# Half products in seven of eight for the last stage of an attention and mixture-of-experts kernel, with a square root by Newton steps

## The chip, the core and the metric

The kernel runs on one core of one Trainium2 chip. The metric is device time in microseconds (us), measured around one launch. A core has five engines with a queue of instructions each: TensorE (PE, the matrix engine; PEld is its weight loading), VectorE (DVE), ScalarE (ACT), GpSimd (POOL) and SyncE (SP, which here only issues DMA transfers). All arithmetic that matters is f32.

## The reference

Input is x of 4 sequences x 1024 tokens x 512 features. The kernel computes one layer in two halves:

```
x = x + layernorm(attention(layernorm(x)))     # linear attention, 16 heads of 32, decay per head, chunks of 128
x = x + layernorm(ffn(layernorm(x)))           # mixture of experts with a shared expert

layernorm(x) = (x - mean) / sqrt(var + 1e-5)
ffn(x):
  shared = (silu(x @ sh_gate.T) * (x @ sh_up.T)) @ sh_down.T       # width 1408
  top 2 of 8 experts by softmax(x @ router.T), weights normalised to sum 1
  cur[e] = (silu(gate_e) * up_e) @ down_e.T                        # width 352, for the chosen tokens
  out = sum of the two cur * weight  +  sigmoid(x @ shared_gate.T) * shared
```

## The kernel before, in words

Tokens are cut into 8 blocks (`n`) of 512 (`TB`), a block into 4 tiles (`j`) of 128. The 512 features are `KC` = 4 slices of 128, the shared expert's width 1408 is `IC` = 11 slices of 128 (`ic`). PE's order of work is written out by hand for the whole kernel (L67); DVE's and ACT's order is written out from L914 on and is chosen by a scheduler before that; POOL's and SP's orders are the program's with the scheduler's changes. Pools of tiles set when a buffer or a PSUM bank can be used again.

The work has five parts, one after the other on PE.

1. **Attention**, blocks 0 to 7 (loop at L614). In the stage of block n PE makes the projections of block n+1 between the chunks of block n, so that they fill its waits. A chunk: scores (`chunk_scores`, products with `sm` made on DVE at L368), output and state (`chunk_out`, bank `pa` from L378 on, `pst` at L400), projection. After chunk 3 comes `attn_residual` (L430): layernorm of the attention's output, on ACT for the scaling (L253), and POOL adds it to `xa` (L435); then `ln2` (L438) and `routing`, whose units (transposes `pt_f`, router logits, choice of experts, scatter of rows to DRAM) are spread over the next block's stage. Transposes `pt_a` (L280) need the normalised next block. In the stage of block 7 there is no next block, and PE does gate and up of the shared expert for block 0 (`shared_units`, L554), whose weights `up_weights` (L139) brings chunk by chunk and whose `xT` waits for the transfer from `xTd`. In front of it `xa` is loaded on the same queue, SP.
2. Down of block 0, and then the shared expert for block 1 (loop from L790, weights by `up_weights`, down weights at L792), during which the experts' weights (`wx`, 23 MB on ACT's queue) are loaded. Both blocks' results go to DRAM (`earlyd`).
3. **Routed tiles**: `NX` = 71 tiles of 128 rows sorted by expert (L881). Each is read from `xg`, transposed, multiplied with its expert's gate and up (L845, 352 columns), turned (L858), multiplied with down (L867), and written to `yg`. In them POOL has nothing to do.
4. **Last stage**: the shared expert for blocks 2 to 7 (L983). For each block 11 chunks of gate and up into banks `pg` and `pu` (4 + 4 f32 products of 512 columns per chunk, L156), silu on ACT, product `h` on DVE (L163), then down for 4 tiles (L1020, 11 f32 products each). All of the weights stay in SBUF (`kept`, `wdr`). PE's first chunk of block 2 lies between the last routed tiles. As a list of `side` work, spread over a block's chunks by count, DVE has `routed_sum` (L941: gathers the two rows of a token from `yg` by POOL, weighs and adds them; L944, L945), `early_block` (L966: the same for blocks 0 and 1, added to `earlyd`, with statistics), and `finish` of the block before (L950: `rstd_of`, scaling at L128, the addition of x1 on POOL at L957, the output).
5. The last block finishes tile by tile on DVE (`finish` with w = 1), the last tile after PE's last product.

`rstd_of` (L106) serves every layernorm: variance plus eps, square root on ACT (L111), reciprocal on DVE (L113), and one Newton step of four small DVE operations (L116 to L119). In the trace an f32 product counts as two instructions on PE.

Of the kernel before, what the change touches and what calls it, by code (L numbers as in the profile page):

```python
# [42 lines left out]
def tile_sandwich(  # L43
# [62 lines left out]
    def rstd_of(mv, name, w=TPB):  # L106

        ve = small.tile([P, w], F32, tag="ve", name=f"ve_{name}")
        nc.vector.tensor_scalar(ve, mv[:, :, 1], EPS, None, ALU.add)
        sd = small.tile([P, w], F32, tag="sd", name=f"sd_{name}")  # L110
        nc.scalar.activation(sd, ve, AF.Sqrt)  # L111
        rs = small.tile([P, w], F32, tag="rs", name=f"rs_{name}")
        nc.vector.reciprocal(rs, sd)  # L113

        t = small.tile([P, w], F32, tag="nt", name=f"nt_{name}")
        nc.vector.tensor_tensor(t, rs, rs, ALU.mult)  # L116
        nc.vector.tensor_tensor(t, t, ve, ALU.mult)
        nc.vector.tensor_scalar(t, t, -0.5, 1.5, ALU.mult, ALU.add)
        nc.vector.tensor_tensor(rs, rs, t, ALU.mult)  # L119
        return rs  # L120
# [18 lines left out]
    def up_weights(n, ic):  # L139

        f = slice(ic * P, (ic + 1) * P)
        wg = wp.tile([P, KC, P], F32, tag="wg", name=f"wg_{n}_{ic}")
        nc.sync.dma_start(wg, shgv[:, :, f])
        wu = wp.tile([P, KC, P], F32, tag="wu", name=f"wu_{n}_{ic}")
        nc.sync.dma_start(wu, shuv[:, :, f])
        return wg, wu
# [7 lines left out]
    def up_half(dst, w, xT):  # L154
        for kc in range(KC):
            nc.tensor.matmul(  # L156
                dst, lhsT=w[:, kc, :], rhs=xT[:, kc, :], start=(kc == 0), stop=(kc == KC - 1)
            )
# [8 lines left out]
    with ExitStack() as ph:  # L167
# [275 lines left out]
        def routing(n, xn2):  # L443
# [4 lines left out]
            pick = small.tile(two, F32, tag="pick", name=f"pick_{n}")  # L448
            both = small.tile([P, TPB, E], BF16, tag="both", name=f"both_{n}")
            pe = small.tile(two, F32, tag="pe", name=f"pe_{n}")  # L450
# [21 lines left out]
        def choice(n, lgT, pick, both, pe):  # L472
# [8 lines left out]
            nc.scalar.activation(sig[:, n, :], lg[:, :, E], AF.Sigmoid)  # L481
# [72 lines left out]
        def shared_units(n):  # L554
# [4 lines left out]
            w, pg = {}, {}  # L559

            def gate(ic):
                w[ic] = up_weights(n, ic)
                pg[ic] = bank(f"pg_{n}_{ic}")
                up_half(pg[ic], w[ic][0], xT)

            def up(ic):
                pu = bank(f"pu_{n}_{ic}")
                up_half(pu, w[ic][1], xT)
                gated(h[:, ic, :], pg[ic], pu, f"{n}_{ic}")
# [159 lines left out]
        for e in range(1, E):  # L729
            less = small.tile([P, 2 * NTB * TPB], F32, tag="less", name=f"less_{e}")  # L730
# [16 lines left out]
    with ExitStack() as ph:  # L747
        ps = ph.enter_context(tc.tile_pool(name="psf", bufs=2, space=PSUM, reuse_waits="tile"))

# [3 lines left out]

        def routed_tiles(mid):
            wxp = mid.enter_context(tc.tile_pool(name="wxp", bufs=1, reuse_waits="tile"))
# [35 lines left out]
            for ic in range(IC):  # L791
                wg, wu = up_weights(n, ic)  # L792
                wd = xk.tile([P, DM], F32, tag="wd", name=f"wd_{n}_{ic}")
                nc.sync.dma_start(wd, shd[ic * P : (ic + 1) * P, :])
                pg = ps.tile([P, TB], F32, tag="pg", name=f"pg_{n}_{ic}")
                up_half(pg, wg, xT)
                pu = ps.tile([P, TB], F32, tag="pu", name=f"pu_{n}_{ic}")
                up_half(pu, wu, xT)
# [79 lines left out]
            ahead_2 = block_ahead(EARLY), [up_weights(EARLY, ic) for ic in range(2)]  # L878
# [21 lines left out]
            xT, ((wg, wu), _) = ahead_2  # L900
            pg = ps.tile([P, TB], F32, tag="pg", name=f"pg_{EARLY}_0")
            up_half(pg, wg, xT)
            hT = turned(NX - 1, last[0])
            pu = ps.tile([P, TB], F32, tag="pu", name=f"pu_{EARLY}_0")
            up_half(pu, wu, xT)
            rows_out(NX - 1, hT, last[1])
            return *ahead_2, pg, pu


        with ExitStack() as mid:  # L910
            first = routed_tiles(mid)
# [6 lines left out]
        )  # L918
        res = ph.enter_context(tc.tile_pool(name="res", bufs=1, reuse_waits="tile"))
        xk = ph.enter_context(tc.tile_pool(name="xk", bufs=2, reuse_waits="tile"))  # L920
        kept = {i: w for i, w in enumerate(first[1])}
        for ic in range(len(kept), IC):
            f = slice(ic * P, (ic + 1) * P)
            wg = res.tile([P, KC, P], F32, tag=f"wg{ic}", name=f"wgr_{ic}")
            nc.sync.dma_start(wg, shgv[:, :, f])
            wu = res.tile([P, KC, P], F32, tag=f"wu{ic}", name=f"wur_{ic}")
            nc.sync.dma_start(wu, shuv[:, :, f])
            kept[ic] = wg, wu
        wdr = res.tile([P, IC, DM], F32, tag="wdr", name="wdr")

        def gather(n, j, k):
            y = xk.tile([P, DM], F32, tag="y", name=f"y_{n}_{j}_{k}", bufs=11)
# [8 lines left out]
        def routed_sum(n, j):  # L941

            y0, y1 = gather(n, j, 0), gather(n, j, 1)
# [4 lines left out]
            return y0  # L948

        def finish(n, acc, x1, mv, j0, w):  # L950

            rs = rstd_of(mv, f"y{n}_{j0}", w)
            for j in range(w):
                a = acc[:, j0 + j, :]
                normed(a, a, mv, rs, j)
                eng = nc.vector if w == 1 else nc.gpsimd
                eng.tensor_tensor(x1[:, j0 + j, :], x1[:, j0 + j, :], a, ALU.add)  # L957
            nc.sync.dma_start(ov[n][:, j0 : j0 + w, :], x1[:, j0 : j0 + w, :])

        def block_tiles(n):  # L960
            x1 = xk.tile([P, TPB, DM], F32, tag="x1", name=f"x1_{n}")
            nc.sync.dma_start(x1, x1d[n])
            acc = xk.tile([P, TPB, DM], F32, tag="acc", name=f"acc_{n}")
            return x1, acc

        def early_block(n):  # L966

            x1, acc = block_tiles(n)
            nc.sync.dma_start(acc, earlyd[n])
            mv = small.tile([P, TPB, 2], F32, tag="mve", name=f"mve_{n}")  # L970

            def add(j):
                y = routed_sum(n, j)
                nc.vector.tensor_tensor(acc[:, j, :], acc[:, j, :], y, ALU.add)
                stats(mv, j, acc[:, j, :], f"e{n}")

            return [lambda j=j: add(j) for j in range(TPB)] + [
                lambda: finish(n, acc, x1, mv, 0, TPB)
            ]

        behind = []
        xT = first[0]
        for n in range(EARLY, NTB):  # L983
            if n + 1 < NTB:
                xT_next = res.tile([P, KC, TB], F32, tag=f"xT{n % 2}", name=f"xT_{n + 1}")
                nc.sync.dma_start(xT_next, xTd[n + 1])
            h = res.tile([P, IC, TB], F32, tag="h", name=f"h_{n}")
            side = behind
            if n - EARLY < EARLY:
                side = side + early_block(n - EARLY)  # L990
            x1, acc = block_tiles(n)
            ys = [None] * TPB

            def own(j):
                ys[j] = routed_sum(n, j)

            side = side + [lambda j=j: own(j) for j in range(TPB)]
            done = 0
            for ic in range(IC):
                wg, wu = kept[ic]  # L1000
                if n == EARLY and ic == 0:
                    pg, pu = first[2:]
                else:
                    pg = ps.tile([P, TB], F32, tag="pg", name=f"pg_{n}_{ic}")
                    up_half(pg, wg, xT)
                    pu = ps.tile([P, TB], F32, tag="pu", name=f"pu_{n}_{ic}")
                    up_half(pu, wu, xT)
                gated(h[:, ic, :], pg, pu, f"{n}_{ic}")
                if n == EARLY and ic == 3:
                    nc.scalar.dma_start(wdr, shd.rearrange("(k p) f -> p k f", p=P))  # L1010

                start = 4 if n == EARLY else 0
# [89 lines left out]
```

## Time and profile before

| | |
|---|---|
| time, median of 3 runs | 2164.21 us (2162.38 to 2167.74) |
| profiled execution: time | 2165.27 us |
| profiled execution: span | 2163.6 us |
| granted TensorE clock | 0.996 |
| PE busy | 2121.8 us, 98% |
| last stage, PE's first to last instruction | 1482.2 to 2155.8 us |
| HBM traffic | 120.46 MB read, 66.59 MB written |

The span is the time from the first to the last instruction in the trace; the execution's own time is 1.7 us longer. A row of the profile reads: line of the source, engine, operation, result tile <- operand tiles, partitions x elements, type, count | busy us, mean ns of one | idle time of the engine right before, and what ended it. A row of PE's waits gives what it waited for, the us in total, how often, and the longest. In a row of the timeline the first two numbers are start and duration in us from the span's start, x8 a run of eight instructions. Matmul durations overlap (they are pipelined), so what an instruction costs is read from the distance of starts, not from its duration.

### The profile page before, as it was taken

The page shows a single profiled execution, that of the slowest core. Times are in us where ns is not written, and L with a number is a line of the kernel's source. Part 1 is how long each engine was busy: PE and PEld are TensorE (multiplying, and loading weights), DVE is VectorE, ACT ScalarE, POOL GpSimd, SP SyncE. Part 2 cuts the span into 40 slices and gives each one's busy share as a digit, 9 for nine tenths or more (in the row PEclk, how much of TensorE's full clock was granted, in tenths as well). Part 3 has the DMA queues.
Part 4 walks back from the last instruction along what each step waited for, and adds up shares of the span by engine and source line. Part 5 has one row for each costly group of instructions (what it writes and reads, how often), then busy time and mean ns, then how long its engine had stood idle before and what let it go on. Part 6 is the DMA issues. An engine that isn't in the chain of part 4 may idle for free.

```text
span 2163.6 us, 23030 instructions
## 1 busy us (share of the span) xinstructions
PE 2121.8 (98%) x8971; PEld 1100.1 (51%) x8971; DVE 597.6 (28%) x1443; ACT 398.0 (18%) x657; POOL 277.8 (13%) x270
## 2 busy tenths in 40 slices
PE   7999999999989999999999999999999999999998
PEld 3555555555545444456655655654444444444443
DVE  2434444544442320111111111111434211212123
ACT  2223323323221210122222221221111000101010
POOL 1122132132130220000000000002322100101010
PEclk9999999999999999999999999999999999999999
DMA  6011221221232349411222221216623020111000
GB/s 226 20 59 59 98 98 59 78 98 59 98 122 73 107 162 358 146 64 66 66 68 64 63 69 64 64 59 197 230 68 103 20 78 20 56 41 54 10 20 20
DMA packets 101851, 188.54 MB, mean 87 GB/s; under 512 B 8849, under 2 KB 42658, under 8 KB 97266
## 3 DMA queue, kind: packets, MB, share of 16 engines
q1 hardware_dynamic: 80498, 128.00, 17.4%
q0 software_dynamic: 11088, 36.00, 4.9%
q10 hardware_dynamic: 10160, 23.07, 3.1%
q8 instruction: 74, 1.21, 0.2%
q14 instruction: 31, 0.25, 0.0%
HBM read 120.46 MB, written 66.59 MB: 86 GB/s over the span
## 4 chain that ended last, share of the span: by engine, by line
PE 87%; DMA 4%; DVE 4%; POOL 2%; SPq 1%; issue 1%; ACT 1%; ACTq 0%; POOLq 0%; DVEq 0%
PE pu L156 12%; PE pg L156 12%; PE pd L1020 10%; PE pq L306 10%; PE pox L867 8%; PE pgx L845 8%; PE pux L845 8%; PE po L424 5%; PE pv L320 2%; PE pd L587 2%; PE ptx L838 1%; POOL xa L435 1%; PE pa L378 1%; DVE sm L368 1%; DMA wx<-in_wdn_dram 1%; PE pst L400 1%
## 5 line engine op out<-in xcount | busy, mean ns | idle before, releaser
L306 PE MATMUL pq<-xnT,wqkv_sb 128*128 128x512 f32 x512 | 233.2, 601 | 0.0
L1020 PE MATMUL pd<-wdr,h 128*128 128x512 f32 x528 | 227.6, 592 | 0.0
L933 POOL DMA_INDIRECT y<-yg,made x64 | 63.5, 992 | 1030.1 <-DMA wur<-in_shu_dram 682.2
L867 PE MATMUL pox<-wx,hT 128*128 (+1 forms) x426 | 194.8, 593 | 0.0
L163 DVE TENSOR_TENSOR h<-sg,pu 128x512 f32<-128x512 f32 x88 | 60.4, 686 | 463.1 <-PE pu L156 405.5
L162 ACT ACTIVATE sg<-pg 128x512 f32<-128x512 f32 x88 | 52.5, 597 | 703.7 <-PE pg L156 633.7
L845 PE MATMUL pgx<-wx,xtT 128*128 x568 | 179.9, 459 | 1.3 <-ACT xtT L840 1.3
L845 PE MATMUL pux<-wx,xtT 128*128 x568 | 179.8, 460 | 0.0
L1020 PEld LDWEIGHTS pd<-wdr,h 128*128 128x128 f32 x528 | 100.5, 190 | 126.1 <-issue 126.1
L156 PE MATMUL pg<-xT,wgr 128*128 128x512 f32 x360 | 161.9, 593 | 0.0
L156 PE MATMUL pu<-xT,wur 128*128 128x512 f32 x360 | 161.9, 592 | 0.0
L306 PEld LDWEIGHTS pq<-xnT,wqkv_sb 128*128 128x128 f32 x512 | 95.4, 192 | 109.2 <-issue 105.8
L845 PEld LDWEIGHTS pgx<-wx,xtT 128*128 128x128 f32 x568 | 107.4, 189 | 80.3 <-issue 33.2
L860 DVE COPY hT<-pth 128x256 f32<-128x256 f32 x71 | 30.2, 425 | 362.6 <-PE pth L858 362.6
L845 PEld LDWEIGHTS pux<-wx,xtT 128*128 128x128 f32 x568 | 102.6, 191 | 45.1
L320 PE MATMUL pv<-wqkv_sb,xnT 128*128 128x512 f32 x256 | 117.3, 601 | 0.0
L424 PE MATMUL po<-wo_sb,aT 128*128 128x512 f32 x256 | 115.7, 595 | 0.0
L156 PEld LDWEIGHTS pg<-xT,wgr 128*128 128x128 f32 x360 | 68.5, 190 | 86.0 <-issue 86.0
L156 PEld LDWEIGHTS pu<-xT,wur 128*128 128x128 f32 x360 | 68.5, 190 | 86.0 <-issue 83.6
L867 PEld LDWEIGHTS pox<-wx,hT 128*128 128x128 f32 (+1 forms) x426 | 75.8, 191 | 68.5 <-issue 68.3
L313 ACT ACTIVATE qk<-pq,bqk_sb 128x512 f32<-128x512 f32 x64 | 44.0, 687 | 261.5 <-PE pq L306 261.5
L350 POOL TENSOR_TENSOR qd<-qk,decq 128x512 f32<-128x512 f32 x28 | 35.5, 1268 | 433.6 <-PE pa L388 407.4
(204 smaller groups left out, 2241.7 us busy)
## 6 DMA issues: line engine op xcount, KB each, us to landing
xt<-xg SPq DMA_DIRECT2D x71, 256.0 KB, 2.6
yg<-yt SPq DMA_DIRECT2D x71, 256.0 KB, 2.0
wx<-in_wgu_dram ACTq DMA_DIRECT2D x8, 1408.0 KB, 12.9
xa<-in_x_dram SPq DMA_DIRECT2D x8, 1024.0 KB, 5.2
x1d<-xa SPq DMA_DIRECT2D x8, 1024.0 KB, 3.9
xTd<-xT SPq DMA_DIRECT2D x8, 1024.0 KB, 4.7
x<-x1d SPq DMA_DIRECT2D x8, 1024.0 KB, 6.0
xn<-in_x_dram SPq DMA_DIRECT2D x7, 1024.0 KB, 6.1
```

Of the source, the lines that this page charges most:

```text
L156: nc.tensor.matmul(dst, lhsT=w[:, kc, :], rhs=xT[:, kc, :], start=(kc == 0), stop=(kc == KC - 1))
L162: nc.scalar.activation(sg, pg, AF.Silu)
L163: nc.vector.tensor_tensor(h, sg, pu, ALU.mult)
L306: nc.tensor.matmul(pq, lhsT=wqkv_sb[:, kc, oc * P : (oc + 1) * P], rhs=xnT[:, kc, :], start=(kc == 0), stop=(kc == KC - 1),)
L313: nc.scalar.activation(qk[:, oc, :], pq, AF.Identity, bias=bqk_sb[:, oc : oc + 1])
L320: nc.tensor.matmul(pv, lhsT=xnT[:, kc, j * P : (j + 1) * P], rhs=wqkv_sb[:, kc, 2 * DM : 3 * DM], start=(kc == 0), stop=(kc == KC - 1),)
L424: nc.tensor.matmul(po, lhsT=aT[:, g, :], rhs=wo_sb[:, g, :], start=(g == 0), stop=(g == G - 1))
L587: nc.tensor.matmul(pd[j], lhsT=h[:, ic, j * P : (j + 1) * P], rhs=wa[:, ic, :] if ic < 8 else wb[:, ic - 8, :], start=(ic == 0), stop=(ic ...
L845: nc.tensor.matmul(dst, lhsT=xtT[:, kc, :], rhs=wx[:, bass.ds(off + (kc * 2 * IM + o), IM)], start=(kc == 0), stop=(kc == KC - 1),)
L867: nc.tensor.matmul(po, lhsT=hT[:w, c, :], rhs=wx[:w, bass.ds(off + (WG + c * DM), DM)], start=(c == 0), stop=(c == 2),)
L933: nc.gpsimd.indirect_dma_start(out=y, out_offset=None, in_=yg[:, :], in_offset=bass.IndirectOffsetOnAxis(ap=made[:, k, n, j : j + 1], axis=0),
L1020: nc.tensor.matmul(pd, lhsT=h[:, ic, j * P : (j + 1) * P], rhs=wdr[:, ic, :], start=(ic == 0), stop=(ic == IC - 1),)
```

## The change

It has six parts.

**Seven products of eight (Winograd's form of Strassen's scheme).** In the last stage each large product is a two by two block product. Gate and up of a chunk: rows are gate and up, the inner cut is features 0 to 255 against 256 to 511, the columns are tokens 0 to 255 against 256 to 511 of the block. Down: rows are token halves, inner halves are chunks 0 to 4 against 5 to 9 with chunk 10 split in its own way, columns are halves of 256 features. Instead of 8 half products there are 7, on sums of blocks; four sums of weights and four sums of tokens (or hidden values) go in, and DVE adds the products up: in `sums` (`q`, `u`, `c2`), and `gb` or `c12` in the end. The first PSUM halves pass through ACT (`copied`). The chunk's instructions are split in `begin`, `middle` and `end`, and chunk i+1's `begin` stands on PE ahead of chunk i's `end`. The scheme uses banks `pa` (3 buffers), `pb` (2), `pd` (3).

**Where the sums are made.** Sums of gate and up weights: on POOL in block 7's attention stage, as the weights pass through (`weight_sums`), written to DRAM as `w8d`; from there every later chunk's weights come in one transfer, in the last stage three buffers ahead of use (`ws`) in place of the weights kept in SBUF. Sums of down weights: on POOL during the routed tiles (`down_weights`), written to `wdd` and read back once. Sums of tokens: on POOL, once per block (`token_sums`), behind the chunks of the block before. Sums of hidden values: on POOL from chunk 5 on (`hidden_sums`), 21 additions a block.

**Square root.** `rstd_of` no longer asks ACT: a first guess by an integer shift and subtraction, and three Newton steps in place of one. Sigmoid becomes exp, addition and reciprocal.

**Gathers first.** A block's eight gathers are issued at the head of its chunks (`gathers`), with 8 buffers in place of 11.

**Finish.** The scaling is made on ACT (Identity with scale and bias) and the addition of x1 on DVE; `finish` is a list of units (`begin` and one per tile) spread like the other side work. In the last block, tiles finish in the order 2, 0, 3, 1 after each pair's products.

**Pools.** The PSUM pool of the tiles closes before the last stage; some small tiles have fewer buffers; the down weights of block 1's loop share the buffers of `xt`.

The program order on PE ahead of the last stage is as before. The diff, cut to what the text speaks of:

```diff
-        sd = small.tile([P, w], F32, tag="sd", name=f"sd_{name}")
-        nc.scalar.activation(sd, ve, AF.Sqrt)
         rs = small.tile([P, w], F32, tag="rs", name=f"rs_{name}")
-        nc.vector.reciprocal(rs, sd)
+        ri = rs.bitcast(I32)
+        nc.vector.tensor_scalar(ri, ve.bitcast(I32), 1, None, ALU.arith_shift_right)
+        nc.vector.tensor_scalar(ri, ri, -1, 0x5F3759DF, ALU.mult, ALU.add)
         t = small.tile([P, w], F32, tag="nt", name=f"nt_{name}")
-        nc.vector.tensor_tensor(t, rs, rs, ALU.mult)
-        nc.vector.tensor_tensor(t, t, ve, ALU.mult)
-        nc.vector.tensor_scalar(t, t, -0.5, 1.5, ALU.mult, ALU.add)
-        nc.vector.tensor_tensor(rs, rs, t, ALU.mult)
+        for _ in range(3):
+            nc.vector.tensor_tensor(t, rs, rs, ALU.mult)
+            nc.vector.tensor_tensor(t, t, ve, ALU.mult)
+            nc.vector.tensor_scalar(t, t, -0.5, 1.5, ALU.mult, ALU.add)
+            nc.vector.tensor_tensor(rs, rs, t, ALU.mult)
         return rs
 ...
+    def up_weights(n, ic, pieces=False):
+        w = wp.tile([P, 4, 2, P], F32, tag="w", name=f"w_{n}_{ic}")
+        if pieces:
+            f = slice(ic * P, (ic + 1) * P)
+            nc.sync.dma_start(w[:, 1:3].rearrange("p a k f -> p (a k) f"), shgv[:, :, f])
+            for i, k in ((0, 0), (3, 2)):
+                nc.sync.dma_start(w[:, i], shuv[:, k : k + 2, f])
+        else:
+            nc.sync.dma_start(w, w8d[ic][:, :4])
+        return w
 ...
+            def weight_sums(ic, w):
+                r = 2 * (ic % 2)
+                s = sums[:, r : r + 2, :].rearrange("p a (b f) -> p (a b) f", b=2)
+                add, sub = ALU.add, ALU.subtract
+                w4 = w.rearrange("p a k f -> p a (k f)")
+                for dst, x, y, op in (
+                    (0, w4[:, 0], w4[:, 3], add),
+                    (1, s[:, 0], w4[:, 1], sub),
+                    (2, w4[:, 1], w4[:, 0], sub),
+                    (3, w4[:, 2], s[:, 1], sub),
+                ):
+                    nc.gpsimd.tensor_tensor(s[:, dst], x, y, op)
+                wd8 = w8d[ic].rearrange("p a k f -> p a (k f)")
+                nc.sync.dma_start(wd8[:, :4], w4)
+                nc.sync.dma_start(wd8[:, 4:], s)
 ...
+        def token_sums(n, xT):
+            t = pre.tile([P, 4, 2, W], F32, tag="xt", name=f"xt_{n}")
+            b11, b12 = xT[:, 0:2, lo], xT[:, 0:2, hi]
+            b21, b22 = xT[:, 2:4, lo], xT[:, 2:4, hi]
+            tt = nc.gpsimd.tensor_tensor
+            tt(t[:, 0], b12, b11, sub)
+            tt(t[:, 1], b22, t[:, 0], sub)
+            tt(t[:, 2], b22, b12, sub)
+            tt(t[:, 3], b21, t[:, 1], sub)
+            return t
 ...
+            down_weights()
+            xT = block_ahead(EARLY)
+            w = up_weights(EARLY, 0)
+            w1 = pre.tile([P, 7, 2, P], F32, tag="w1", name="w1")
+            nc.sync.dma_start(w1, w8d[1][:, 1:])
+            sums_2 = token_sums(EARLY, xT)
 ...
+        def weights(n, ic):
+            w = res.tile([P, 7, 2, P], F32, tag="ws", name=f"ws_{n}_{ic}", bufs=3)
+            nc.sync.dma_start(w, w8d[ic][:, 1:])
+            ws[n, ic] = w
 ...
+        def copied(name, pa):
+            tmp = wp.tile([P, 4, W], F32, tag="w", name=f"tmp_{name}")
+            nc.scalar.copy(tmp[:, 0], pa[:, lo])
+            return tmp
 ...
+        def sums(name, tmp, pb, pd):
+            p1, q, u = tmp[:, 0], tmp[:, 1], tmp[:, 2]
+            nc.vector.tensor_tensor(q, p1, pb[:, lo], add)
+            nc.vector.tensor_tensor(u, q, pb[:, hi], add)
+            c2 = res.tile([P, 2, W], F32, tag="c2", name=f"c2_{name}", bufs=2)
+            nc.vector.tensor_tensor(
+                c2,
+                pd.rearrange("p (a w) -> p a w", a=2),
+                u.unsqueeze(1).to_broadcast([P, 2, W]),
+                add,
+            )
+            return c2.rearrange("p a w -> p (a w)"), q, tmp[:, 3]
 ...
+            def begin():
+                product(pa[:, lo], both(a11, xT[:, 0:2, lo]))
+                return copied(f"{n}_{ic}", pa)
+            def middle(tmp):
+                product(pb[:, lo], both(s2, t[:, 1]))
+                product(pb[:, hi], both(s3, t[:, 2]))
+                product(pd[:, lo], both(a22, t[:, 3]))
+                product(pd[:, hi], both(s1, t[:, 0]))
+                c2, q, gb = sums(f"{n}_{ic}", tmp, pb, pd)
+                product(pa[:, lo], both(a12, xT[:, 2:4, lo]), start=False)
+                nc.scalar.activation(sg[:, lo], pa[:, lo], AF.Silu)
+                return c2, q, gb
+            def end(c2, q, gb):
+                product(pd[:, hi], both(s4, xT[:, 2:4, hi]), start=False)
+                nc.vector.tensor_tensor(gb, q, pd[:, hi], add)
+                nc.scalar.activation(sg[:, hi], gb, AF.Silu)
+                nc.vector.tensor_tensor(h[:, ic, :], sg, c2, ALU.mult)
 ...
+            def one(j):
                 a = acc[:, j0 + j, :]
-                normed(a, a, mv, rs, j)
-                eng = nc.vector if w == 1 else nc.gpsimd
-                eng.tensor_tensor(x1[:, j0 + j, :], x1[:, j0 + j, :], a, ALU.add)
-            nc.sync.dma_start(ov[n][:, j0 : j0 + w, :], x1[:, j0 : j0 + w, :])
-        def block_tiles(n):
-            x1 = xk.tile([P, TPB, DM], F32, tag="x1", name=f"x1_{n}")
-            nc.sync.dma_start(x1, x1d[n])
+                nc.scalar.activation(
+                    a, a, AF.Identity,
+                    bias=scale["nm"][:, j : j + 1], scale=scale["rs"][:, j : j + 1],
+                )
+                nc.vector.tensor_tensor(x1[:, j, :], x1[:, j, :], a, ALU.add)
+                if j == w - 1:
+                    nc.sync.dma_start(ov[n][:, j0 : j0 + w, :], x1)
+            return [begin] + [lambda j=j: one(j) for j in range(w)]
 ...
+        def hidden_sums(s, left, hs, i):
+            tt = nc.gpsimd.tensor_tensor
+            if i == HC:
+                tt(left, hs(2 * HC)[:, hi], hs(2 * HC)[:, lo], sub)
+                return
+            a11, a12, a21, a22 = hs(i)[:, lo], hs(HC + i)[:, lo], hs(i)[:, hi], hs(HC + i)[:, hi]
+            tt(s[:, 0, i], a21, a22, add)
+            tt(s[:, 1, i], s[:, 0, i], a11, sub)
+            tt(s[:, 2, i], a11, a21, sub)
+            tt(s[:, 3, i], a12, s[:, 1, i], sub)
 ...
+            stt = nc.vector.scalar_tensor_tensor
+            stt(b, c2, sb, ys[p + 2][0], ALU.mult, ALU.add)
+            done(p + 2)
+            stt(a[:, lo], pa[:, lo], sa, ys[p][0][:, lo], ALU.mult, ALU.add)
+            nc.vector.tensor_tensor(c12, q, pd[:, hi], add)
+            stt(a[:, hi], c12, sa, ys[p][0][:, hi], ALU.mult, ALU.add)
+            done(p)
 ...
+            for ic in range(first, IC + 1):
+                if ic < IC:
+                    begin, middle, next_end = up_chunk(n, ic, xT, t, h)
+                    tmp = begin()
+                if end is not None:
+                    end(*sent)
+                    if ic - 1 >= HC:
+                        hidden_sums(s, left, hs, ic - 1 - HC)
+                    if ic + 2 < IC:
+                        weights(n, ic + 2)
+                    elif n + 1 < NTB:
+                        weights(n + 1, ic + 2 - IC)
+                if ic < IC:
+                    sent, end = middle(tmp), next_end
+                if n == EARLY and ic == 4:
+                    nc.scalar.dma_start(wdr, wdd)
+                while done < len(side) * max(0, ic + 1 - idle) // (IC - idle) and done < len(side):
                     side[done]()
                     done += 1
+            if n + 1 < NTB:
+                t = token_sums(n + 1, xT_next)
```

## The prediction

> **What bounds the kernel now.** First the page's busy shares and slices, to see whether one engine sets the time.
>
> ```profile
> PE 2121.8 (98%) x8971; PEld 1100.1 (51%) x8971; DVE 597.6 (28%) x1443; ACT 398.0 (18%) x657; POOL 277.8 (13%) x270
> ...
> PE   7999999999989999999999999999999999999998
> ...
> PEclk9999999999999999999999999999999999999999
> ```
>
> PE is busy in every slice and its clock is granted throughout. So only matmul time and PE's waits count; then come the waits, to see what PE has ever waited for:
>
> ```profile
> PE pt_a L292 <- DVE xn L128: 11.4, 1, 11.4
> PE pg L156 <- DMA xT<-xTd: 6.3, 1, 6.3
> PE pt_a L280 <- DVE v L327: 6.3, 5, 1.6
> PE pa L378 <- DVE sm L368: 5.0, 1, 5.0
> PE pu L156 <- DMA wu<-in_shu_dram: 1.9, 2, 1.1
> ```
>
> All of them lie in the first 870 us; the last stage (1482.2 to 2155.8) has none. Its length is its instructions. The chain's last part says what one costs:
>
> ```profile
> 2004.73 37.77 PE pd L1020 x88
> 2118.03 37.78 PE pd L1020 x88
> ```
>
> 88 instructions in 37.77 us are 429 ns each at 512 columns (each f32 product is two instructions). The two starts are 113.3 us apart: 37.77 of down and 75.5 of gate and up, 11 chunks of 6.86.
>
> **The products.** A chunk's 16 instructions of 512 columns become 28 of 256 (7 half products in place of 8), a block's down 88 become 156. No row has 256 columns. The weight loads' starts give the nearest ones on both sides:
>
> ```profile
> 216.24 0.97 PEld L400 LDWEIGHTS pst<-v,kd 128*128 128x128 f32 x8 [0.20 <-issue]
> 217.12 0.30 PEld L320 LDWEIGHTS pv<-wqkv_sb,xnT 128*128 128x128 f32 x2
> ```
>
> ```profile
> 1004.14 2.53 PE L845 MATMUL pgx<-wx,xtT 128*128 x8
> 1006.51 0.49 PE L858 MATMUL pth<-ident,hx 128*128 128x128 f32 x3
> ```
>
> Eight at 128 columns take 0.88 us (110 ns each), eight at 352 take 2.37 (296). 110, 296 and 429 lie on one line, 109 + (columns - 128) x 0.833; it gives 215.7 ns at 256. Bounds: 110 and 296. A load is 190 ns, yet at 128 columns loads pass at 110 ns apart, so they overlap; I take 215.7. A chunk: 28 x 0.2157 = 6.04 against 6.86, -0.82; 65 chunks (the first one stays whole): -53.6. Down: 156 x 0.2157 = 33.65 against 37.77, -4.1; six: -24.6. Together **-78.2**. Each ns on the 256-column pitch is 65 x 28 + 6 x 156 = 2756 instructions x 1 ns = 2.8 us.
>
> The Trainium skill ("TensorE: Matmul & The Clock Gate", Back-to-back issue gap) says that in a stream of load and matmul pairs both set the spacing, 81 ns at 128 columns where the matmul alone would have 56. By that half again on 110 ns would show at 128 columns; the 110 ns row lies on the line of the wide ones, so the trace does not bear it out. With the same share on 215.7 ns the sum would stand some 300 higher.
>
> **What the products now wait for.** Before, PE needed nothing of DVE inside a chunk. Now chunk i+1's `s4` product adds into bank pd after DVE's `c2` of that chunk has read it, and silu of the second half waits for `gb`. PE gives DVE from `middle`'s last pd product (t = 0): `c2` 0.18 to 0.87, then a12's product (0.86) and the next `begin` (0.86) cover it, s4 at 1.73. `gb` 0.43, silu 0.39 and h 0.69 end at 5.2 with q and u for the next, whose c2 must start by 6.9. So DVE may have about 3.6 us of side work per chunk. Side units by rows of the trace:
>
> ```profile
> 1538.39 3.82 DVE L128 TENSOR_SCALAR acc<-acc,mve,rs_y 128x512 f32<-128x512 f32 x4
> 1542.13 0.68 DVE L163 TENSOR_TENSOR h<-sg,pu 128x512 f32<-128x512 f32 x1
> 1542.73 0.89 DVE L944 TENSOR_SCALAR y<-y,share 128x512 f32<-128x512 f32 x1
> 1543.66 1.64 DVE L945 SCALAR_TENSOR_TENSOR y<-y,share,y 128x512 f32<-128x512 f32 x1
> ```
>
> An early unit is 0.48 + 0.75 + 0.69 + 0.69 + 0.18 = 2.8 (medians); `finish.begin` is 16 small dependent operations at 0.2, 3.2; an own sum 1.2; one normalised tile 0.7 behind an ACT 0.8. Block 2 has 13 units in 7 chunks: chunk 5 gets two early units (5.6, over by 2.1), chunk 6 one and `begin` (over by 2.5). Block 3 has 18 in 11: over by 1.4, 2.1, 1.2. Blocks 4 to 7 have nine, none over. 9.3, and 0.17 at each block's last chunk, 1.0: **10.3 with clean durations**.
>
> But the rows above show 1.64 for a 0.75 operation: DVE is held while POOL adds (L957), and this goes for L128 by its medians and maxima:
>
> ```profile
> L128 DVE TENSOR_SCALAR acc<-acc,mv,rs_y x24: 541/547/1493, 1605.2 to 2159.0; 128x512 f32<-128x512 f32 x24
> ```
>
> From chunk 5 on POOL makes 21 `hidden_sums` of 0.74 a block (line between 1.27 at 512 columns and 0.21 at 9). If each delayed DVE once by 0.9 in the five overfull chunks (some 8 operations) it would be +7. I take +2.7 of that: **+13**, between 0 and 20. The Trainium skill ("SBUF — State Buffer", Who interferes with whom) has the rule: an operation of VectorE with two SBUF inputs and one of GpSimd exclude each other, and the one that comes second blocks fully. The rows agree (547 against 1493), and by it rival C below follows.
>
> **Start of the last stage.** SP's queue after the last tile holds ws_2 (0.9 MB), a yg write, ws_3, xT, acc and x1 (1 MB each), ws_4, and POOL's eight gathers (2.1 MB) run at the same time: 8.3 MB before chunk 4's weights are in. The machine's 16 engines move some 400 GB/s in this place of before (1514 to 1530), so 21 + 2 us; chunk 4 is needed 17.3 after. Stall 5.6, and 0.9 as bank pa is that of the last tile's output, still being copied: **+6.7** (0 if the transfers of x1 come later; 10 at 350 GB/s).
>
> **POOL at the start of down.** After the last `hidden_sums` group (2.96) come the next block's `token_sums` (4 x 1.27) and the gathers, and only then `left` (0.74), which the first pb product needs 7.8 us after the last chunk. Blocks 4 to 6 reach 7.2, 2 and 3 with more gathers 9.2. 2 x 1.4, up to 3 when held by DVE, and 0.4 x 4: **+5** (0 to 8).
>
> **Square root by Newton.** Ten more small dependent operations, less the ACT turn and the reciprocal: net 8 x 0.2 = 1.6, in every normalisation. ACT's table loads (42, 1283 ns) go to 6, but were off PE's path: 0. Attention's block changes are the place that pays:
>
> ```profile
> 212.31 0.17 DVE L109 TENSOR_SCALAR ve_o<-mvo 128x4 f32<-128x4 f32 x1
> 212.38 0.68 DVE L368 TENSOR_TENSOR sm<-sc,dmask 128x512 f32<-128x512 f32 x1
> ...
> 215.23 0.81 PEld L378 LDWEIGHTS pa<-sm,v 128*32 128x32 f32 x32 [0.76 <-DVE nt_o L118]
> ```
>
> PE takes pa just as the last sm ends (slack 0.2), and pt_a already waits 1.0 to 1.6 here. In the changed program's order seven of the small operations stand ahead of the first sm: pa 1.4 later, then pt_a 1.6 more: 3.0 at five changes, +15. At 0 to 1 the 5.0 us accident of sm behind POOL goes and 4.3 comes: with what stood after it, -1.5. At 6 to 7 the loads of xa and xT wait for nm_f, 4.05 later: +4.05 onto the 6.3 wait. At the start the last tile's normalisation: +3.6. **+21.2** (10 to 27, as DVE's order can hide half of each or add).
>
> **Tail.** Before, 7.8 us lie between PE's end and the end. Now the last pair gives two tiles; DVE finishes tile 3 (16 small operations, ACT 0.8, an add) before it begins tile 1: its last add ends 14.75 after pd's sixth product, PE 4.3 after. Out 3.3: 13.7. **+5.9** (0 to 8).
>
> **Hidden.** Weights of block 1's loop come in one piece of 4 KB packets: the 1.9 of wu waits go, **-2**. The 44 weight sums in block 7's stage make one SP chain per chunk (load, write, sums) of 6 us under PE's 6.9; with no cover each chunk would pay 1 to 3. Down's sums (33 transfers, 23 additions) are on POOL during the tiles, where it is idle: 0. Gathers first, sigmoid by exp: 0.
>
> **Sum** on the profiled execution, 2165.27 (span 2163.6; 1.1 above the median, 2164.2): -78.2 + 13 + 6.7 + 5 + 21.2 + 5.9 - 2 = -28.4, **2137**.
>
> **Rivals.** (A) The forecast, 0.55: 2120 to 2150.
> (B) The covers hold: side work, transfers and POOL's chain cost nothing. For it: DVE is 28% busy, POOL 13%, and PE never waited in this stage. Against it: the chunk's slack is counted from clean rows. -78.2 + 21.2 + 5.9 - 2: 2112, 0.20.
> (C) DVE and POOL exclude each other all through chunks 5 to 10 and the Newton steps: rows for it are 162 to 1249 ns at L119 and 547 to 1493 at L128; against it, POOL's work per block is 21 operations in 33 us. 20 more: 2157, 0.15 (a third of it faster, half the same).
> (D) Weight loads bind at 256 columns, where a load of 190 ns is near the matmul's 216: the point that decides is 2137 + 2.756 x ns = 2165, a pitch of 226 ns. At 255, halfway to the 352-column row, 2756 x 39 = +108: 2245. The 110 ns row speaks against it: 0.10.
> That the last stage still makes eight products is out: the changed program has 2756 instructions of 256 columns there.
>
> **The numbers.** The likeliest is 2137. Range 2106 to 2164: below lies a part of B, above a part of C and all of D. A measurement here can tell about 0.3% (2157.7 and 2170.7) from no change. Faster: 0.55 + 0.20 + 0.05 = 0.80; same 0.08; slower 0.10 + 0.02.
>
> **What would show it.** Right: PE's waits on pt_a grow by some 3 us each; 156 instructions of down in 33.7 us; PE waits in blocks 2 and 3 alone; ws_4 late by 5. Wrong: a pitch over 222 ns at 256 columns, waits at every chunk of blocks 4 to 7 (C), none at all (B), a startup shift other than 3.6.

## The result, and the profile after

The changed kernel takes 2152.3 us (median of 6 runs) beside 2166.0 of the kernel before: a ratio of 0.9937, 95% interval 0.9921 to 0.9954. It is 13.7 us faster where 28.4 had been forecast. The profiled execution took 2150.3 us, its span 2148.6.

The time by stages says where the other half went. A row of the windows is: stretch and its length, busy time of the five engines, granted clock, share of the DMA engines, GB/s. The kernel before, from the first projection to block 7's first gate product, and the last stage:

```profile
15.60:637.20 621.60, 603.87 (x4393) 330.44 (x4393) 278.30 (x705) 181.92 (x290) 138.23 (x125) 0.99 0.23 86
...
1482.20:2155.80 673.60, 673.33 (x1569) 298.20 (x1567) 173.78 (x317) 60.68 (x91) 102.14 (x92) 1.00 0.22 72
```

The same stretches after, and the tail:

```profile
15.70:668.80 653.10, 619.49 (x4392) 335.06 (x4393) 315.03 (x906) 154.13 (x251) 143.66 (x133) 0.98 0.23 85
...
1513.90:2136.10 622.20, 602.56 (x2757) 524.43 (x2755) 335.92 (x724) 99.42 (x238) 187.02 (x210) 0.99 0.49 168
2136.10:2148.60 12.50, 0.00 (x0) 0.00 (x0) 6.92 (x29) 1.63 (x2) 0.00 (x0) 0.67 0.18 63
```

The last stage is 51.4 shorter (53.5 forecast), the tail 4.8 longer (5.9 forecast). The attention is 31.5 longer with the same PE instructions (4393 in the record before, 4392 after). PE's waits after:

```profile
PE pt_a L296 <- DVE v L343: 19.7, 9, 3.4
PE pa L1034 <- DMA ws<-w8d: 10.9, 3, 6.5
PE pg L168 <- DMA xT<-xTd: 10.2, 1, 10.2
...
PE pd L1034 <- DVE c L1061: 4.9, 3, 2.4
PE pa L394 <- DVE sm L384: 3.6, 14, 0.3
...
PE pa_d L1034 <- DVE h L1097: 2.3, 2, 1.5
PE pb_d L1034 <- POOL s_left L1163: 1.4, 1, 1.4
```

pt_a waits 19.7 us in place of 6.3, and the last stage, which had one wait of 0.3, has four kinds: for the weights ws, for the sums c, for the hidden values h and for their last sum s_left. What the waits don't show is the clock. The timeline of PE at the change from block 1 to 2, after:

```profile
226.54 1.47 PE L296 MATMUL pt_a<-ident,xn 128*128 128x128 f32 x12
230.77 0.66 PE L296 MATMUL pt_a<-ident,xn 128*128 128x128 f32 x4 [2.75 <-DVE v L343]
231.26 5.39 PE L440 MATMUL po<-wo_sb,aT 128*128 128x512 f32 x8
```

After an idle of 2.75 us eight products of 512 columns take 5.2 us from the first to the next group's start, where eight at 429 ns take 3.4: four run at 850 ns. The granted clock of that place is 0.50 (the first column is the stretch, the third number from the right the clock):

```profile
233.00:235.00 2.00, 2.00 (x4) 0.90 (x3) 0.00 (x0) 0.00 (x0) 0.00 (x0) 0.50 0.98 362
```

Putting PE's instructions of the two traces side by side (their order is the same up to the last stage), the shift at each change of blocks splits so (us; slow is what a distance of two instructions grew by beyond its idle time):

| change of blocks | pa behind sm | more idle at pt_a behind v (6 to 7: at pg behind xT) | slow instructions | sum |
|---|---|---|---|---|
| 1 to 2 | 1.5 | 1.7 | 1.8 | 5.0 |
| 2 to 3 | 1.4 | 2.3 | 1.8 | 5.4 |
| 3 to 4 | 1.4 | 1.8 | 2.0 | 5.2 |
| 4 to 5 | 1.3 | 2.3 | 3.4 | 7.0 |
| 5 to 6 | 1.3 | 1.7 | 1.6 | 4.6 |
| 6 to 7 | 1.3 | 3.9 | 0 | 5.2 |

With -1.2 at 0 to 1 and 0.4 up to the first projection that is 31.6. The column of slow instructions fits the record of the granted clock: it stands at 0.50 for 3.41 us at four of these changes and for 6.83 us at 4 to 5, and half of these times is 1.7 and 3.4.

### The profile page after: what moved, and what is told of

It is laid out like the page before. It is cut to its first block, busy times and chain, and to the rows that moved or that the text cites. A ratio compares the mean times of both kernels' runs of the same rounds, so it can differ in the third digit from the quotient of the medians.

```text
span 2148.6 us, 26594 instructions
## 1 busy us (share of the span) xinstructions
PE 2066.3 (96%) x10159; PEld 1330.4 (62%) x10159; DVE 809.9 (38%) x2128; ACT 405.3 (19%) x757; POOL 432.9 (20%) x491
## 4 chain that ended last, share of the span: by engine, by line
PE 84%; DVE 7%; DMA 3%; POOL 3%; issue 2%; ACT 1%; SPq 0%; ACTq 0%; DVEq 0%; POOLq 0%
PE pq L322 11%; PE pox L952 9%; PE pgx L930 8%; PE pux L930 8%; PE pd L1034 7%; PE po L440 5%; PE pb L1034 5%; PE pa L1034 4%; PE pd_d L1034 4%; PE pg L168 3%; PE pu L168 3%; PE pb_d L1034 3%; PE pa_d L1034 2%; PE pv L336 2%; DMA ws<-w8d 2%
## 5 line engine op out<-in xcount | busy, mean ns | idle before, releaser
L1168 POOL TENSOR_TENSOR s<-h 128x256 f32<-128x256 f32 x30 | 21.8, 728 | 669.6 <-PE pox L952 531.9
L440 PE MATMUL po<-wo_sb,aT 128*128 128x512 f32 x256 | 124.9, 634 | 0.1
L1034 PE MATMUL pb<-xt,ws 128*128 128x256 f32 x512 | 121.5, 380 | 0.0
L1034 PE MATMUL pd<-xt,ws 128*128 128x256 f32 x512 | 121.0, 379 | 0.0
L1034 PEld LDWEIGHTS pb<-xt,ws 128*128 128x128 f32 x512 | 98.0, 191 | 13.6
L1034 PEld LDWEIGHTS pd<-xt,ws 128*128 128x128 f32 x512 | 97.3, 190 | 13.2
L384 DVE TENSOR_TENSOR sm<-sc,dmask 128x512 f32<-128x512 f32 x128 | 80.8, 682 | 18.9 <-PE sc L374 18.9
L440 PEld LDWEIGHTS po<-wo_sb,aT 128*128 128x128 f32 x256 | 50.6, 205 | 57.4 <-issue 56.7
L983 DVE TENSOR_TENSOR hx<-sgx,pux 128x352 f32<-128x352 f32 x71 | 37.0, 521 | 129.6 <-PE pux L930 129.6
```

Source lines behind the costliest of these rows:

```text
L384: nc.vector.tensor_tensor(t, scs[s], dmask[:, s], ALU.mult)
L440: nc.tensor.matmul(po, lhsT=aT[:, g, :], rhs=wo_sb[:, g, :], start=(g == 0), stop=(g == G - 1))
L983: nc.vector.tensor_tensor(h, sg, pu, ALU.mult)
L1034: nc.tensor.matmul(dst, lhsT=a, rhs=b, start=(start and i == 0), stop=(i == len(pairs) - 1), skip_group_check=True,)
```

## The experiments

Theory N: Newton's steps on DVE cost the attention its 31.6. Theory K: part of it is PE's clock, which falls after the longer idle. Theory Q and R: the last stage's start pays for the order and the row sizes of its transfers. "Attention" below is the time from PE's first projection product to block 7's first gate product: 621.6 and 619.8 in two executions of the kernel before, 653.2 and 651.0 after.

On two of the chips the kernel before took 2186 and 2187 us in place of 2166; the runs there (sqrt_attention, newton_alone, pe_kept_busy, weights_ahead, down_in_pieces, weights_first) are compared with that, and with each other by stages.

**The old square root in the attention.** Each place chooses by name:

```diff
+    def rstd_of(mv, name, w=TPB):
+        pick = rstd_newton if name[0] == 'y' else rstd_sqrt
+        return pick(mv, name, w)
```

> The changed kernel, with the old square root (ACT, reciprocal, one Newton step) in the attention's three normalisations and Newton's three steps in the last stage only. Theory N: the 31.6 us that PE comes late to block 7's first gate product (668.8 against 637.2) are the added small operations on DVE, ahead of the bias addition that frees the bank of pt_a. Then that product is back at 637 +- 2, PE's waits on pt_a at 1.0 to 1.6, and the time is 2152.3 - 31.5 = 2121. Rival S: DVE's order moved for another reason of the change (sigmoid by exp, fewer small buffers, weight sums): the product stays after 655 and the time above 2140.

2139.9 us, 0.9785 (0.9769 to 0.9802) of before's 2186.1. Attention 642.6, beside 664.7 in the weights-ahead kernel of the same chip, which has the changed kernel's attention: 22.1 less. On this chip that leaves block 7's first gate product at 659.6, in the range that rival S had named, and the time at the edge of its range. What puts it out is the all-mended run below: with the same square roots on a chip where before takes 2166, the attention takes 619.5, as in the kernel before. That 22.1 isn't 31.5 belongs to the chip (last section).

**Newton alone in the kernel before**: the same helper with `name[0] != 'y'`.

> The kernel before, with Newton's three steps in the attention's normalisations and nothing else changed. Theory N: block 7's first gate product at 668 +- 3 and 2166 + 31.5 = 2197. Rival S: less than half of the shift is there, 2180 or less.

2209.7 against 2186.1, 1.0105 (1.0088 to 1.0121): 23.6 us slower, with no other part of the change in it. It agrees with the 22.1 on this chip, and 2197 was missed because before itself was 20 slower.

**PE kept busy while it waits.**

```diff
-                for j in range(TPB):
-                    nc.tensor.transpose(
+                for _ in range(5 if kc == 2 and name[0] == "a" else 1):
+                    for j in range(TPB):
+                        nc.tensor.transpose(
```

> The changed kernel, with the third unit of pt_a transposes made five times over in its own bank (16 more transposes of 0.11 us, 1.8 us, in the 2.75 to 3.4 us in which PE waits for the fourth unit's bank). Theory K: after an idle of 2.7 us or more PE runs some 2 to 6 instructions at half speed (0.85 us in place of 0.43; 20 of them at six changes, 8.5 us), and below 2.5 us it doesn't: the idle falls to 1.0 to 1.6, the slow instructions go, 2152.3 - 8.5 = 2144. Rival: the slow instructions have another cause (the transfers or the operations that run beside them): the same 20 remain, 2152. If the idle is not real slack, 6 x 1.8 more: 2163.

2156.2, 0.9861 of 2186.1; attention 656.1 beside 664.7. To have it on a chip where before takes 2166, it was run again:

> The kernel in which PE repeats pt_a's third unit while it waits for the fourth's bank, beside kernels of the same chip. Theory K: 2152 - 8.5 = 2143 where before takes 2166, and no instruction of 0.85 us behind pt_a. Rival: the 8 us that lay between it and the weights-ahead kernel up to block 7 came from that pair's chip: 2152.

2147.0 beside 2165.8, 0.9911 (0.9894 to 0.9928); attention 644.1, 7 to 9 less than the changed kernel. The same change of blocks:

```profile
227.12 3.22 PE L297 MATMUL pt_a<-ident,xn 128*128 128x128 f32 x28
231.36 0.66 PE L297 MATMUL pt_a<-ident,xn 128*128 128x128 f32 x4 [1.01 <-DVE v L344]
231.85 3.70 PE L441 MATMUL po<-wo_sb,aT 128*128 128x512 f32 x8
```

28 transposes in place of 12, the bank comes free at the same point, and the eight products behind take 3.5 us. No instruction behind pt_a was slow in any of the six changes, against 17 to 20. K holds: added work made the stage faster. The whole gained 5 of the 8.5 expected; the other idles kept their slow instructions (2.1 behind h of block 1's loop, none in the trace of after_again).

**Two steps in place of three.** `for _ in range(2)`; the result is less exact by the third step.

> The changed kernel with two Newton steps in place of three in every square root (the result is less exact by the third step). Theory N with the clock: a step is four dependent operations, 0.8 us; at each change of blocks pt_a's idle falls from 2.75 to 3.4 to about 2.0, which is under the point where the clock falls (2.5 to 2.7), so 0.8 and 1.4 go at five changes, 0.8 at 6 to 7 twice, 0.8 at the start, 0.8 in the tail twice: -14, and no slow instructions after pt_a. Rival without the clock: 0.8 only, -7, and the slow instructions remain.

2134.2, 0.9855 (0.9838 to 0.9871): 17.6 less than the changed kernel on this chip (2151.8); attention 639.5. pt_a's idle fell to 2.3 to 2.55, not to 2.0, and behind it the clock fell at four changes of six: 9 slow instructions. So the point of the clock is not at 2.5 to 2.7, as the expectation had it.

**One chain at a time.** `name[0] != 'o'` and `name[0] != 'f'` in the helper above choose Newton.

> The changed kernel with the old square root in the normalisation of the attention's output alone (rs_o), Newton's steps in the other two. Theory N, in two chains: at a change of blocks rs_o stands ahead of sm (pa later by 1.4) and rs_f ahead of the v that frees pt_a's bank. With rs_o short, pa's 1.4 goes at six changes, and rs_f's chain begins 1.2 earlier, so pt_a's idle falls to 1.6 to 2.2 and the slow instructions mostly go: -8.4 - 5 x 1.2 - 6 = -20, 2132. Rival: only rs_f counts (the wait moves from pa to pt_a): -8 or less, 2144.

> The changed kernel with the old square root in the second layernorm alone (rs_f), Newton's steps for rs_o and rs_a. Theory N: pa stays 1.4 late at each change, pt_a's idle falls by 1.6 to 2.2 to 1.0 to 1.6, the slow instructions behind it go: 5 x (1.6 + 1.4) + 1.6 at block 7's xT = -17, 2135; with the run for rs_o the two sum to more than the 32 of both, since either alone takes the idle below the point of the clock. Rival: the two chains overlap on DVE and rs_f alone brings less than 8.

2137.2 and 2129.3 beside 2165.8; attention 636.5 and 628.7, against 651 to 653 with all of them long and 619.5 with all short (the all-mended run below). The waits, of the run with rs_o short and then with rs_f short:

```profile
PE pt_a L316 <- DVE v L363: 12.6, 5, 2.8
...
PE pa L414 <- DVE sm L404: 5.0, 1, 5.0
```

```profile
PE pt_a L316 <- DVE v L363: 8.7, 6, 2.3
...
PE pa L414 <- DVE sm L404: 3.6, 14, 0.3
```

With rs_o short the 14 small waits of pa are gone and the old 5.0 us accident of the change from 0 to 1 is back; pt_a still idles 2.3 to 2.8 with 11 slow instructions. With rs_f short pt_a idles 0.9 to 1.8 from block 2 on, and nothing is slow there. The two gains, 15.6 and 23.4, sum to 39, more than the 32 of all together, as expected: either takes idle away that the other would have taken. That rs_o alone would bring pt_a below the clock's point was wrong.

**The start of the last stage.** First the order of transfers and the down weights together:

```diff
-        for ic in range(2, 4):
+        for ic in range(2, 5):
             weights(EARLY, ic)
...
-                if n == EARLY and ic == 4:
-                    nc.scalar.dma_start(wdr, wdd)
+                if n == EARLY and 4 <= ic < 4 + HC:
+                    a = (ic - 4) * 7 * W
+                    z = a + 7 * W if ic < 3 + HC else DW + 4 * W
+                    nc.sync.dma_start(wdr[:, a:z], wdd[:, a:z])
```

> The changed kernel, with three weight chunks of the last stage (ws) asked for ahead of xT, acc and x1, and the 5.1 MB of down weights in five pieces on SP's queue behind the chunks' own weights in place of one transfer on ACT's queue. Theory Q: PE's two waits on ws (4.2 and 6.5 us, and 15 instructions at half speed, 3.2) come from the order of the transfers: they go, -14, 2138. Rival B: the engines' throughput binds in the first 45 us (some 400 GB/s), and the wait moves to another chunk or to the start of down: 2146 or more.

2157.7, 0.9867 of 2186.1. The last stage on PE is 613.7 beside 622.7 in the kernel of the same chip that kept its start: 9.0 of the 14. Its waits:

```profile
PE pd L1034 <- DVE c L1061: 9.9, 5, 3.2
...
PE pa L1034 <- DMA ws<-w8d: 1.0, 1, 1.0
```

The wait for ws is 1.0, and 5.0 us behind c have come up in block 2, which had lain under it. Then each half alone: the order only, and the down weights only in five transfers on ACT's queue.

> The changed kernel with three ws chunks asked for ahead of xT, acc and x1, and the down weights left as they are. Theory Q: the 4.2 us wait at chunk 4 (and 1.5 to 1.7 of slow instructions) goes, the 6.5 us wait stays: -5, 2147. Rival: the queues are full from the start of the stage for 40 us, so the later wait grows by what the first one loses: 2151 or more.

> The changed kernel with the 5.1 MB of down weights on ACT's queue as before, issued at the same place, but in five transfers, four of 896 KB and one of 1408 KB, so that a partition's row is 7 KB (11 KB in the last) in place of 39 KB. Theory R: between queues the DMA engines take turns packet by packet (71, 73 and 71 packets of three queues in the same 9 us of the changed kernel), so the queue with rows of 39 KB gets five times what the one with rows of 7 KB gets; with equal rows ws gets a third to a half of some 400 GB/s, 896 KB in 5 to 7 us in place of 14: PE's 6.5 us wait falls under 1.5 and the slow instructions behind it (1.9) go: -7, 2145. Rival V: the volume of the 15 us decides (5.1 MB beside ws), whatever the rows: the wait stays above 4, 2150 or more.

2160.8 and 2166.5 beside 2187.4 (0.9879 and 0.9901); last stages 617.7 and 620.6, against 621.7 to 623.6 in the seven profiles, of all chips, that keep this start with three steps in the last stage. With the order, chunk 4's wait went from 4.2 to 0.9 without slow instructions, and chunk 7's stayed (7.3). With the pieces, chunk 4's stayed (3.9) and chunk 7's is 0.2; but 4.0 us of c came up in its place with 1.7 us of slow instructions, so 1 to 3 us were left of 7. The volume of the transfers is the same as in the changed kernel, so it was the rows that made the long wait. Why the rows matter is in the DMA view of the changed kernel for 1549 to 1558 (packets, MB, share):

```profile
q10 hardware_dynamic: 71, 2.84, 73.6%
q1 hardware_dynamic: 73, 0.52, 14.1%
q0 software_dynamic: 71, 0.26, 7.1%
```

Nearly equal numbers of packets, of 39,936, 7168 and (but for seven) 4096 bytes: q10 (the down weights) gets 315 GB/s and q1 (ws) 58. The Trainium skill ("DMA: Bandwidth & Descriptors", Queues, rings and completion order) says that each engine goes round the queues packet by packet; the trace agrees, 71, 73 and 71.

**All mended.** The old square root in the attention (also for the last block's tiles, scaled on DVE there), the transfers of the weights-ahead run, token sums behind the first pair.

> The changed kernel with the old square root in the attention and for the last block's single tiles (which DVE also scales itself), the weights of the last stage ahead of the other transfers, the down weights in five pieces, and the next block's token sums behind the first pair's products in place of ahead of down. Theory: the parts lie in different stages and add: 31 less in attention (23 on the slower chip), 9 at the last stage's start, 1.6 at s_left, 4 in the tail: 45 less than the changed kernel where before takes 2166 (2107), 37 less where it takes 2186 (2127). Rival: PE's other waits take their place (sums c behind side work in block 2, h at down), and less than half of the last stage's 10.6 comes.

2109.4 beside 2166.3, 0.974 (0.9724 to 0.9756); the changed kernel took 2151.8 on the same chip. Attention 619.5, last stage 613.9, tail 9.9. So 31.4 of the 42.4 lie in the attention, 7.8 in the last stage (10.6 expected; s_left's 1.4 stayed, since POOL still had it behind the token sums), 2.7 in the tail.

**Side work in another order**, s_left on DVE, and the token sums ahead of down again:

```diff
+            if n == EARLY:
+                order = (0, 1, 9, 2, 10, 3, 11, 4, 12, 5, 6, 7, 8)
+                side = [side[i] for i in order]
+            elif n == EARLY + 1:
+                order = (0, 1, 2, 5, 3, 4, 6, 14, 7, 8, 15, 16, 17, 9, 10, 11, 12, 13)
+                side = [side[i] for i in order]
```

> As all_mended, with s_left made on DVE behind h in place of POOL, token sums back ahead of down, and the side work of blocks 2 and 3 in another order, so that no chunk gets two early units or an early unit with the root of finish (each early unit is paired with a sum of 1.2 us or stands alone). Theory S: PE's 9.9 us behind c at five chunks come from the chunk's budget of 3.6 us of DVE work: at most 4.1 to 4.4 is now asked of one, so 3 or less is left, and the 1.4 at s_left goes: -8, 2101. Rival P: the waits come from POOL holding DVE (an operation of 0.75 took 1.1 to 1.64 there), which another order doesn't change: -1.4 only, 2108.

2101.0 beside 2165.8, 0.9696 (0.968 to 0.9712): the fastest of all, 64.8 us under the kernel before. The profiled execution took 2106.1, the slowest of the four. Its waits, in which s_left no longer stands:

```profile
PE pd L1054 <- DVE c L1081: 5.1, 4, 1.5
PE pa L1054 <- DMA ws<-w8d: 2.3, 1, 2.3
PE pa_d L1054 <- DVE h L1117: 0.2, 1, 0.2
```

That is 8.4 less than the all-mended run on another chip with the same kernel before, as theory S had it, although 5.1 and not 3 are left behind c: 4.8 went there, 1.4 at s_left and 2.1 at h, and 1.1 came up at ws. The three edits were not tried apart.

**Both kernels again on one chip.**

> The changed kernel once more, on the same chip as the next three, so that stages can be compared on one chip: on the chip of the first four experiments the kernel before took 2186 us in place of 2166, because DVE's first sm of a block waited 1.6 to 3.4 us for PE's signal although the products had long ended. Theory C (the chip delays that signal, in either kernel, so part of Newton's delay lies in its shadow there): if before takes 2186 again, the change gives 2163 to 2167 (-20 to -23); if it takes 2166, the change gives 2152 again (-14). Rival: the change is worth the same -14 on both: 2172 beside 2186.

> The kernel before, for its stages on the same chip. Theory C: if it takes 2186, all of the 20 us lie in the attention blocks 1 to 6 (block 7's first gate product at 657 in place of 637), at pa behind sm. Rival: they are spread over the whole span by the clock or the transfers (1% in each stage).

2151.8 (0.9939, 0.9922 to 0.9956) and 2165.6: this chip was of the usual kind, so the two gave the first result once more, and theory C of the slower chips was not tried.

## Why the prediction was right and wrong

- **Products: right.** The 256-column pitch is 216.0 ns (2242 of 2755 distances), 215.7 forecast. In the chain of waits of the changed kernel:

```profile
1806.10 5.18 PE pb_d L1034 x24
```

  24 in 5.18 us is 215.8 ns. Rival D is dead: loads of 190 ns hide behind 216.
- **Square root by Newton, +21.2: the step that failed.** It was 31.6. The mechanism was right in every place (pa 1.3 to 1.5, forecast 1.4; pt_a 1.7 to 2.3, forecast 1.6; xT 3.9, forecast 4.05), and its terms were mis-sized. Above all, no term stood for the clock: 10.6 us of slow instructions at five changes, as much as the whole miss of 10.4. The profile of before had shown slow products behind idles of 5 us and more and none behind 1.6; nothing lay between, and I priced the longer idle as idle alone. Behind v, five changes cost 9.8 in place of 8.0, and at 6 to 7 pa's 1.3 was left out. In the other direction, the 3.6 at the start didn't come: before, the third tile of x was there at 8.1 and after at 5.5, which is the transfer's chance. Over all runs the first projection starts at 15.3 to 19.0 us with Newton's steps there and at 15.6 to 16.9 without. That the smaller errors cancel is luck.
- **Start of the last stage, +6.7: mis-sized.** It measured 15.5. ws_4 was late by 4.2 (5.6 forecast from the sum of bytes); some 4 of slow instructions behind the waits and 6.5 of a second wait were missing. I had checked that the down weights land in time, and not what their rows of 39 KB do to the queue beside them.
- **Side work, +13: 6.4.** Block 3's three stalls are 0.9, 2.4 and 1.6 (1.4, 2.1, 1.2 forecast), the last chunks' are 0.1 each (0.17 forecast), block 2's 4.6 lay under the wait for ws and appeared as 5.0 when that went. The 2.7 for POOL's holding of DVE was not needed at these places.
- **Start of down, +5: 4.8**, by other shares: s_left 1.7 in block 2 and 0.3 in block 3, h 1.1 and 1.8. By the timeline, h was late because DVE's last sums were stretched while POOL made token sums. DVE in the all-mended run, beside POOL (the changed kernel has the same durations at 1589.9 to 1593.5):

```profile
1551.60 1.71 POOL L850 TENSOR_TENSOR xt<-xT 128x512 f32<-128x512 f32 x1
...
1552.11 1.48 DVE L1136 TENSOR_SCALAR y<-y,share 128x512 f32<-128x512 f32 x1
1553.27 1.45 POOL L852 TENSOR_TENSOR xt<-xT 128x512 f32<-128x512 f32 x1
1553.63 1.64 DVE L1137 SCALAR_TENSOR_TENSOR y<-y,share,y 128x512 f32<-128x512 f32 x1
```

  0.48 became 1.48 and 0.75 became 1.64, and POOL's 1.27 became 1.45 to 1.71: rival C's mechanism, at the end of a block's chunks and hardly elsewhere in the stage. The prediction set L128's 547 and 1493 beside a rule for operations with two SBUF inputs; but L128, like the operation of 0.48 here, reads one wide tile, and only the one of 0.75 reads two. Both kinds were stretched, so these rows don't bear out the condition of two inputs.
- **Block 1's weights, -2: right, and given back.** The waits for wu went; PE waits 2.3 longer for an h in that loop, whose silu on ACT starts at 850.3, right behind the issue of an expert's transfer at 849.9, by the timeline; its gate product had ended at 844.8. That ACT's queue of transfers held the silu was not tried.
- **Tail, +5.9: 4.8.**

The terms of the last stage were off by +8.8, -6.6 and -0.2, which nearly cancel, so its total came out by luck as much as by the mechanism. Rival B fell with the waits of that stage. On the profiled execution (15.0 faster) the forecast missed by 13.4: 10.4 in the Newton step, 2.1 in the last stage, 2.1 from block 1's loop on, -1.1 in the tail.

## What to carry to other kernels

When PE is the bound, a few small operations of another engine ahead of the one that frees a bank cost more than their own time: price the idle, and then the slow products behind it. Moving work from an idle engine (ACT) to one in whose queue PE's next bank stands is not free because the work is small. A transfer that has time enough can still starve its neighbour if its rows are longer: cut it to rows like the neighbour's. When a wait is taken away, look for what had lain under it.

## What the runs showed of the hardware

- The granted clock falls earlier than I had taken it to. Over the sixteen profiled executions, idles of PE from 0.5 to 1.9 us that stood alone were never followed by a granted clock of 0.50 (149 cases), from 2.2 to 2.6 us 11 times in 24, from 2.6 to 3.0 24 in 25, from 3.0 to 3.6 21 in 28, from 3.6 to 5 always (9). Up to the last stage each such stretch of the clock's record lasts 3.41, 6.83 or 10.24 us, and cost 1.6 to 3.4 us at the changes of blocks above. Short idles in a row count too: on two chips (next point) PE idled four times within some 3 us, for 1.1 to 1.5 us and then three times for 0.3, with two small products between, and the clock fell behind 15 of these 36 groups. The Trainium skill ("TensorE: Matmul & The Clock Gate", What's actually happening) puts the fall after an idle window of about 3.4 us that runs freely; here 2.3 us were enough in half the cases, so the measurement decides.
- Two chips took 20 us more for the same kernel before. In the four profiles from the first of them, DVE's first sm of blocks 2 to 7 starts 4.0 to 4.2 us after the last sc product ended, whatever DVE did before (4.1 to 4.4 in the two profiles of the second); on the other chips it is 0.7 with the old rs_o and 2.1 to 2.4 with Newton's steps. In the run with the old square root:

```profile
213.30 3.70 PE L356 MATMUL pv<-wqkv_sb,xnT 128*128 128x512 f32 x8
...
217.37 0.69 DVE L404 TENSOR_TENSOR sm<-sc,dmask 128x512 f32<-128x512 f32 x1 [3.19 <-PE pv L356]
```

  DVE sat idle for 3.2 us, and the first pa product came 4.75 us behind the last sc product in place of 3.56. The signal that DVE waits for comes from PE and, by the trace, arrives only after the pv products. Why stays open. It makes up the 20 us: beside the all-mended run, which has the same square roots in the attention on a usual chip, PE is 3.2 to 3.7 later at each of the six changes of blocks, 20.6 in all, with short idles and at times the clock's fall behind them. (The kernel before itself was not profiled there.) It also fits that Newton cost 22 to 24 there and 32 elsewhere, since its first seven operations lay in that wait.
